# The last block of a mixture-of-experts feed-forward: its rows leave memory, and a gate matrix takes them to their tokens

## The chip, the cores and the metric

The kernel runs on one core of a Trainium2 chip. A core has a matrix engine (TensorE, PE in the profile; PEld is its loading of the stationary operand), a vector engine (VectorE, DVE), an activation engine (ScalarE, ACT), a general engine that also issues the indirect transfers (GpSimd, POOL), and a queue that issues plain transfers (SyncE, SP). Each engine works through its own list of instructions in order; between engines there are semaphores. The metric is the device time of one execution in microseconds; a time is given as the median of several executions. A profiled execution also leaves a trace, in which every instruction has its start, its length and what it waited for.

## What is computed

Two layers work on an image batch of 4 images with 384 channels and 32x32 pixels, that is 1024 tokens for each image. Layer 0 is a convolution-like attention with relative positions, followed by a small feed-forward. Layer 1 is a depthwise convolution, followed by a mixture of experts; only this end matters here:

```python
t = _to_tokens(x)                      # (4, 1024, 384)
t = t + _L1_ffn_ref(_ln_t(t), ...)
x = _from_tokens(t, x)                 # back to (4, 384, 32, 32)

def _L1_ffn_ref(x, gate_w, gate_b, w1, b1, w2, b2):      # 4 experts, top 2
    probs = softmax(x @ gate_w + gate_b)
    masked = probs with only the two largest kept, divided by (their sum + 1e-9)
    h = gelu(einsum('bsd,edh->ebsh', x, w1) + b1)        # 384 -> 1536
    y = einsum('ebsh,ehd->ebsd', h, w2) + b2             # 1536 -> 384
    return einsum('bse,ebsd->bsd', masked, y)
```

So each token's result is its own value plus gate0 times the row that its first expert made of it, plus gate1 times the row of its second expert. The kernel computes only the two chosen experts of each token.

## The kernel before, in words

Layer 0 (the first 1700 us) is left out here; the change touches nothing of it.

**Sorting tokens to experts.** For each image, `gates` and `scatter` choose two experts per token, give each pair of token and expert a slot in the expert's list in memory, and write the normalised token row there (`xs_d`). The lists are cut into blocks of 128 rows. There are 67 blocks (`ALL`), in four groups of 13, 16, 16 and 22 that follow the four images: a group starts when the image that completes its blocks has been sorted.

**Blocks.** `blocks(g, more)` runs the blocks of a group, one after the other. For each block, GpSimd gathers its 128 rows (`xg`, line 1265) and, where they change, the expert's weights (`w`, line 1284); TensorE turns the rows (`turn`, line 1278). Then come 12 steps `ff`: three products of 128x128 with the first weight (line 1316), GELU on ScalarE (line 1319), and, two steps later, one product of 128x384 with the second weight into the sum `py` (line 1294). Every float32 product is two instructions on TensorE. When the twelfth second product is done, VectorE adds the bias (`yo`, line 1297) and SyncE writes the 128 rows to `y_d` in memory (line 1299). Since the second products run two steps late, block k's `yo` is made during the second step of block k+1.

**Work beside the blocks.** After each step `blocks` calls `more(g, k)`, which issues pieces of other work. In the last group, from block 6 on (`NOT_LAST`), this is `combine(range(3))`: it works out for every token of all four images in which rows of `y_d` its two results lie (`result_rows`, which writes them as unsigned integers to `images[b]["pos"]`), and then finishes the first three images in pieces of 256 tokens, 12 in all.

**Bringing results back to tokens.** For a piece, `results` issues four gathers on GpSimd (line 1355; two for each half of 128 tokens, one per expert choice, into `rows` buffers, of which there are 16); `weigh` multiplies the first by its gate on ScalarE (line 1367) and adds gate times the second on VectorE (line 1368); `finish` turns the result by six transposes of 128x128 on TensorE (line 1344), adds it to the image on VectorE in two instructions (line 1345), and writes 256 tokens to the output (line 1346).

**The end.** `combine([B - 1])`, the fourth image, runs after all 67 blocks. Its 16 gathers are issued at once and may read any row of `y_d`, so the first of them waits until the last block's rows have been written. The image itself (`xbs[3]`) is still in on-chip memory.

**What sets the order.** The code is a trace of instructions; a planner orders each engine's list afterwards by the times of a model, free to move what is ready earlier ahead of what was written earlier. `pin` takes that freedom away: it keeps an instruction behind whatever was written just before it for the same engine. The tiles of a pool with the same tag share a fixed number of buffers (`bufs`); an instruction that needs one waits until its last reader is done. In PSUM there are two banks of tag `m`, three of `h`, two of `y` and one of `t`.

Of the kernel before, what the change touches and what calls it, by code (L numbers as in the profile page):

```python
# [53 lines left out]
MAXB = B * N // BLK  # L54
OUTSIDE = 1e6
# [749 lines left out]
def result_rows(nc, small, image, pieces):  # L805
# [18 lines left out]
    nc.vector.tensor_copy(image["pos"], row)  # L824

# [78 lines left out]
def rest_phase(tc, cst, x, ao_d, ins, xs_d, y_d, x2_d, out):  # L904
# [9 lines left out]
    with ExitStack() as es:  # L914
# [344 lines left out]
        def blocks(g, more):  # L1259
# [32 lines left out]
            def second(k, ff, hs, w, py):  # L1292
                o = WB + ff % FH * C
                nc.tensor.matmul(py, hs, w[:, o : o + C], start=(ff == 0), stop=(ff == NF - 1))  # L1294
                if ff == NF - 1:
                    yo = hid.tile([P, C], F32, tag="yo", name="yo", bufs=2)
                    nc.vector.tensor_tensor(yo, py, w[:, WB + FH * C :], ALU.add)  # L1297
                    n = (g["start"] + k) * BLK
                    nc.sync.dma_start(y_d[n : n + BLK, :], yo)
# [30 lines left out]

        def combine(bs):
# [4 lines left out]
            y_rows = y_d if end else y_d[: (groups[-1]["start"] + NOT_LAST) * BLK]  # L1336
            pieces = [p for g in groups for p in g["pieces"]]

# [9 lines left out]
            def results(b, n0):  # L1348

                zs = []  # L1350
                for j in range(2):
                    ys = [new_row() for _ in range(2)]
                    for i, y in enumerate(ys):
                        index = images[b]["pos"][:, n0 // P + j, i : i + 1]
                        nc.gpsimd.indirect_dma_start(y, None, y_rows, bass.IndirectOffsetOnAxis(ap=index, axis=0))
# [8 lines left out]
            def weigh(b, n0, zs):  # L1364
                for j, (z, y) in enumerate(zs):
                    gate = images[b]["gate"][:, n0 // P + j, :]
                    nc.scalar.activation(z, z, AF.Copy, scale=gate[:, 0:1])
                    nc.vector.scalar_tensor_tensor(z, y, gate[:, 1:2], z, ALU.mult, ALU.add)
                return [z for z, _ in zs]

            if not end:
                for b in (*bs, B - 1):
                    result_rows(nc, small, images[b], pieces)
                    yield 3.0, 0.0
            todo = [(b, n0) for b in bs for n0 in range(0, N, w)]
            ahead = {}
            for i, (b, n0) in enumerate(todo):
                for more in todo[i : i + (len(todo) if end else 2)]:
                    if more not in ahead:
                        ahead[more] = results(*more)  # L1380
                zs, xr = ahead[b, n0]
# [5 lines left out]
                finish(b, n0, xr, zs)  # L1387
# [101 lines left out]
        def more(g, k):  # L1489
# [4 lines left out]
            spend(g.get("combined", iter(())))  # L1494
            while clock[0] < clock[1] and spend(todo):
# [7 lines left out]
        for _ in groups[-1]["combined"]:  # L1503
            pass
        for _ in combine([B - 1]):
# [103 lines left out]
```

## Time and profile before

| what | value |
|---|---|
| time, three executions | 3046.1, 3054.85 and 3057.67 us; median 3054.85 |
| the profiled execution's own time | 3037.78 us |
| its span in the profile | 3036.0 us, so 1.78 us lie around it |
| busy share of the span | PE 96%, DVE 65%, ACT 45%, POOL 38% |
| one block of the last group, without other work beside it | 16.3 us (from one `yo` to the next, 2972.81 and 2989.11) |
| the second last block's `yo` starts | 2989.11 us |
| the last block's `yo` starts | 3003.56 us |
| from there to the end | 32.4 us |

The page of a profile has a table of busy times, a strip of 40 slices of the span, the chain of work that ended last, and groups of like instructions. In a group the columns are: source line, engine, operation, output and inputs with their shapes, count, total busy time and mean length in ns, idle time of the engine before it and what ended that. A query for stretches of time gives, for each stretch, its length, the busy time and count of each engine, the clock that TensorE was granted (1.00 is full speed), and the transfers.

### The profile page before, as it was taken

To read this page: it belongs to the slowest core of one execution; us is meant where nothing else is said; L and a number is where in the kernel's file an instruction comes from. 1 tells how busy PE (TensorE), PEld (TensorE's weight loads), DVE (VectorE), ACT (ScalarE), POOL (GpSimd) and SP (SyncE) were. 2 spreads that over 40 slices of the span, in tenths; PEclk is the share of its full clock that TensorE was granted. 3 is DMA by queue.
4 is the path that set the end of the run, shared out by engine and by line. 5 is a ranking of instruction groups with operands and counts; after the bars stand their busy time and mean duration, and the time that the engine had idled before them with its cause. 6 is when DMAs were issued, how large, how long until landed. Compare 5 with 4: busy or idle time off the path is not lost.

```text
span 3036.0 us, 63460 instructions
## 1 busy us (share of the span) xinstructions
PE 2914.2 (96%) x25391; PEld 2017.5 (66%) x25391; DVE 1960.5 (65%) x3577; ACT 1370.9 (45%) x2833; POOL 1156.4 (38%) x1123
## 2 busy tenths in 40 slices
PE   9998999999999999999999789999999999999996
PEld 4555777777777777777533347776577777778774
DVE  3237787778787878787578869999999740001101
ACT  1116667666666666666422232332343242233332
POOL 1115656464747373747400123252024322115412
PEclk9999999999999999999999879999999999999998
DMA  4346667667666666665500304734144056366752
GB/s 156 138 139 216 153 217 163 217 160 213 169 206 176 205 168 205 168 209 156 195 21 35 135 27 159 273 144 156 65 159 158 28 189 235 134 254 245 281 190 73
DMA packets 274568, 500.56 MB, mean 165 GB/s; under 512 B 135632, under 2 KB 204112, under 8 KB 266592
## 3 DMA queue, kind: packets, MB, share of 16 engines
q1 hardware_dynamic: 185376, 269.93, 28.8%
q0 software_dynamic: 37792, 202.68, 18.0%
q10 hardware_dynamic: 51104, 23.89, 3.9%
q8 instruction: 200, 3.28, 0.5%
q14 instruction: 96, 0.79, 0.1%
HBM read 543.58 MB, written 152.37 MB: 229 GB/s over the span
## 4 chain that ended last, share of the span: by engine, by line
PE 74%; DVE 11%; issue 8%; DMA 3%; POOL 2%; ACT 2%; SPq 0%; ACTq 0%; POOLq 0%; DVEq 0%
PE e_ps L1316 14%; PE y_ps L1294 13%; PE t_ps L408 7%; PE av_ps L221 7%; PE sc_ps L221 7%; DVE xb L1104 6%; PE tabq_ps L221 5%; PE qk_ps L174 4%; PE a_ps L418 3%; PE v_ps L185 2%; PE tv_ps L221 2%; PE tap_ps L1152 1%; DVE extra L400 1%; PE row_ps L87 1%; POOL bias L351 1%
## 5 line engine op out<-in xcount | busy, mean ns | idle before, releaser
L1316 PEld LDWEIGHTS e_ps<-xT,w 128*128 128x128 f32 x4824 | 655.1, 192 | 213.6 <-issue 11.5
L351 POOL TENSOR_TENSOR bias<-b,s 128x416 f32<-128x416 f32 (+24 forms) x656 | 659.8, 1042 | 183.3 <-DMA s<-sd 165.1
L1316 PE MATMUL e_ps<-xT,w 128*128 128x128 f32 x4824 | 669.1, 276 | 10.6 <-DVE xb L1045 4.0
L1294 PE MATMUL y_ps<-w,eh 128*128 128x384 f32 x1608 | 649.1, 489 | 5.3 <-ACT eh L1319 5.0
L1104 DVE SCALAR_TENSOR_TENSOR xb<-img,pack,xb 128x1024 f32<-128x1024 f32 (+1 forms) x539 | 634.6, 1243 | 0.0
L1319 ACT ACTIVATE eh<-e_ps,w 128x128 f32<-128x128 f32 x804 | 293.8, 367 | 706.1 <-PE e_ps L1316 694.5
L1284 POOL DMA_INDIRECT w<-in_w,row x134 | 170.5, 1273 | 720.5 <-PE y_ps L1294 273.3
L400 DVE TENSOR_REDUCE extra<-arow 128x32 f32<-128x32 f32 (+24 forms) x768 | 381.0, 554 | 8.6 <-ACT arow L389 4.9
L379 DVE CUSTOM_DVE_ANT_0 arow<-sc_ps,bias 128x1024 f32<-128x1024 f32 x256 | 312.5, 1221 | 103.6 <-issue 55.1
L389 ACT ACTIVATE arow<-arow,nm 128x1024 f32<-128x1024 f32 x256 | 302.2, 1181 | 77.9 <-DVE nm L379 68.9
L408 PEld LDWEIGHTS t_ps<-ident,arow 128*128 128x128 f32 x2048 | 220.0, 142 | 174.5 <-ACT aT L409 100.5
L409 ACT COPY aT<-t_ps 128x512 f32<-128x512 f32 x512 | 278.4, 603 | 92.6 <-PE t_ps L408 92.1
L408 PE MATMUL t_ps<-ident,arow 128*128 128x128 f32 x2048 | 281.8, 281 | 16.7 <-ACT arow L389 16.7
L1297 DVE TENSOR_TENSOR yo<-y_ps,w 128x384 f32<-128x384 f32 x67 | 37.1, 554 | 386.1 <-PE y_ps L1294 386.1
L221 PE MATMUL sc_ps<-kk,qs 48*32 48x512 f32 x4096 | 277.5, 605 | 7.3 <-DVE nm L379 6.0
L1294 PEld LDWEIGHTS y_ps<-w,eh 128*128 128x128 f32 x1608 | 247.7, 192 | 17.8 <-ACT eh L1319 7.1
L221 PEld LDWEIGHTS av_ps<-aT,vb 128*64 128x64 f32 x4096 | 222.3, 137 | 51.3 <-ACT aT L409 42.1
L316 DVE STREAM_TRANSPOSE b<-tabk_ps 128x480 f32<-128x480 f32 x256 | 218.5, 982 | 35.1 <-PE tabk_ps L221 35.0
L221 PE MATMUL av_ps<-aT,vb 128*64 128x128 f32 x4096 | 237.7, 274 | 0.0
L221 PE MATMUL tabq_ps<-tab,kq 48*128 48x480 f32 x512 | 219.5, 578 | 4.7 <-ACT st L320 2.6
L221 PE MATMUL tabk_ps<-tab,kq 48*128 48x480 f32 x512 | 222.6, 582 | 0.0
L221 PEld LDWEIGHTS tabq_ps<-tab,kq 48*128 48x128 f32 x512 | 148.6, 296 | 44.4 <-ACT aT L409 5.4
(210 smaller groups left out, 3138.1 us busy)
## 6 DMA issues: line engine op xcount, KB each, us to landing
sd<-st SPq DMA_DIRECT2D x128, 480.0 KB, 2.5
s<-sd SPq DMA_DIRECT2D x256, 240.0 KB, 4.0
xs_d<-zero SPq DMA_DIRECT2D x64, 384.0 KB, 4.4
tvw<-in_tv SPq DMA_DIRECT2D x120, 192.0 KB, 4.3
y_d<-yo SPq DMA_DIRECT2D x67, 192.0 KB, 2.1
qk_d<-qk_sb POOLq DMA_DIRECT2D x48, 256.0 KB, 2.4
qs<-qk_d SPq DMA_DIRECT2D x256, 48.0 KB, 3.0
kq<-qk_d ACTq DMA_DIRECT2D x56, 192.0 KB, 4.5
```

The costliest lines, as they stand in the source:

```text
L221: ins = nc.tensor.matmul(*args, **kw)
L316: turn = nc.vector.transpose(b2.rearrange("p e y x -> p x (e y)")[:, i + j], ps[:, j, : SPAN * IMG])
L351: nc.gpsimd.tensor_tensor(bias[:, y0:y1, :], bass.AP(b2.tensor, b2.offset + (e * IMG + y0) * IMG, [list(b2.ap[0]), [(step * IMG + 1) * IMG ...
L379: nc.vector.tensor_tensor_reduce(s["flat"], ps.rearrange("p h n -> p (h n)"), s["bias"].rearrange("p y x -> p (y x)"), -SCALE, BIG, ALU.ad ...
L389: nc.scalar.activation(s["flat"], s["flat"], AF.Exp, bias=s["nm"], scale=-1.0, accum_out=dn[:, y % YT : y % YT + 1])
L400: pin(nc.vector.tensor_reduce(ex[:, i, :], a[:, p0:p1, :].rearrange("p y x -> p x y"), AX.X, ALU.add))
L408: pin(nc.tensor.transpose(pt[:, j, :], s["flat"][:, k0 : k0 + P], ident))
L409: pin(nc.scalar.copy(aT[:, 4 * g : 4 * g + 4, s["y"] % YB, :], pt))
L1104: ins_ = nc.vector.scalar_tensor_tensor(acc[:, k, y0:y1], img[:, k, dy + y0 : dy + y1, dx : dx + IMG], w7[:, k, dy, dx : dx + 1], acc[:, k ...
L1294: nc.tensor.matmul(py, hs, w[:, o : o + C], start=(ff == 0), stop=(ff == NF - 1))
L1316: nc.tensor.matmul(ph, w[:, o : o + P], xT[k][:, c, :], start=(c == 0), stop=(c == KC - 1))
L1319: nc.scalar.activation(hs, ph, AF.Gelu, bias=w[:, o : o + 1])
```

## The change

The rows of the last block (block 66, rows from `LAST` = 8448 on) are no longer written to `y_d`. They stay on chip as `yo`, and reach their tokens of the fourth image through a matrix product.

- `choose` builds the matrix `picked` (128 block rows by 1024 tokens). For each 128 tokens, VectorE compares the two row numbers of each token, less `LAST`, with 0 to 127 and multiplies by the gate (two instructions of 128x128), adds the two (one more), TensorE turns the result (one transpose), and ScalarE copies it from PSUM into the part of `img` that the convolution no longer needs. It is advanced by one step for each of the 12 pieces of the first three images.
- `kept` holds the fourth image's gates, with zero where the row lies in the last block.
- The 16 gathers of the fourth image read `y_d[:LAST]` with a check on the bound (an index beyond it moves nothing). They are issued when the second last block has handed out its `yo`, that is, during the second step of the last block, no longer after the last block.
- `weigh` of the fourth image uses `kept`, and both its instructions are pinned.
- `close` takes the place of `finish` for the fourth image: three products of `yo` (128x128) with 256 columns of `picked`, then six products of the weighed rows with the identity that add to the same three banks (of tags `m`, `h` and `y`), three additions of 128x256 on VectorE, and the write.

```diff
+LAST = (ALL - 1) * BLK
@@ result_rows
     nc.vector.tensor_copy(image["pos"], row)
+    return row
@@ blocks, second
                     nc.vector.tensor_tensor(yo, py, w[:, WB + FH * C :], ALU.add)
                     n = (g["start"] + k) * BLK
-                    nc.sync.dma_start(y_d[n : n + BLK, :], yo)
+                    g["result"] = k, yo
+                    if n < LAST:
+                        nc.sync.dma_start(y_d[n : n + BLK, :], yo)
@@ new
+        kept = small.tile([P, nj, 2], F32, tag="e_kept", name="e_kept", bufs=1)
+        picked = img.rearrange("p k y x -> p (k y x)")[:, :N]
+        def choose(row):
+            gate = images[B - 1]["gate"]
+            rel = small.tile([P, nj, 2], F32, tag="e_rel", name="e_rel", bufs=1)
+            nc.vector.tensor_scalar_add(rel, row, -float(LAST))
+            nc.vector.tensor_scalar(kept, rel, 0.0, None, ALU.is_lt)
+            nc.vector.tensor_tensor(kept, kept, gate, ALU.mult)
+            line = small.tile([P, P], F32, tag="e_line", name="e_line", bufs=1)
+            for n0 in range(0, P, MAXB):
+                nc.vector.tensor_scalar_add(line[:, n0 : n0 + MAXB], pc["blocks"], float(n0))
+            yield
+            last = None
+            for j in range(nj + 1):
+                if last is not None:
+                    ps = ps_m.tile([P, P], F32, tag="m", name="pick_ps")
+                    nc.tensor.transpose(ps, last, ident)
+                    nc.scalar.copy(picked[:, (j - 1) * P : j * P], ps)
+                if j < nj:
+                    hits = [small.tile([P, P], F32, tag=f"e_hit{i}", name="e_hit") for i in range(2)]
+                    for i, hit in enumerate(hits):
+                        nc.vector.tensor_scalar(
+                            hit, line, rel[:, j, i : i + 1], gate[:, j, i : i + 1], ALU.is_equal, ALU.mult
+                        )
+                    last, other = hits
+                    nc.vector.tensor_tensor(last, last, other, ALU.add)
+                yield
@@ combine
-            y_rows = y_d if end else y_d[: (groups[-1]["start"] + NOT_LAST) * BLK]
+            y_rows = y_d[:LAST] if end else y_d[: (groups[-1]["start"] + NOT_LAST) * BLK]
+            def close(b, n0, xr, zs):
+                yo = groups[-1]["result"][1]
+                sums = []
+                for c, (pool, tag) in enumerate(((ps_m, "m"), (ps_h, "h"), (ps_y, "y"))):
+                    ps = pool.tile([P, TOK], F32, tag=tag, name="out_ps", **({"bufs": 2} if tag == "y" else {}))
+                    nc.tensor.matmul(
+                        ps[:, :w], yo[:, c * P : (c + 1) * P], picked[:, n0 : n0 + w], start=True, stop=False
+                    )
+                    sums.append(ps)
+                for j in range(2):
+                    for c, ps in enumerate(sums):
+                        nc.tensor.matmul(
+                            ps[:, j * P : (j + 1) * P], zs[j][:, c * P : (c + 1) * P], ident,
+                            start=False, stop=(j == 1),
+                        )
+                for c, ps in enumerate(sums):
+                    nc.vector.tensor_tensor(xr[:, c, :], xr[:, c, :], ps[:, :w], ALU.add)
+                nc.sync.dma_start(out[b, :, n0 : n0 + w].rearrange("(k p) n -> p k n", p=P), xr)
@@ combine, results
-                        nc.gpsimd.indirect_dma_start(y, None, y_rows, bass.IndirectOffsetOnAxis(ap=index, axis=0))
+                        bound = {"bounds_check": LAST - 1, "oob_is_err": False} if end else {}
+                        nc.gpsimd.indirect_dma_start(
+                            y, None, y_rows, bass.IndirectOffsetOnAxis(ap=index, axis=0), **bound
+                        )
@@ combine, weigh
-                    nc.scalar.activation(z, z, AF.Copy, scale=gate[:, 0:1])
-                    nc.vector.scalar_tensor_tensor(z, y, gate[:, 1:2], z, ALU.mult, ALU.add)
-                    gate = images[b]["gate"][:, n0 // P + j, :]
+                    gate = (kept if end else images[b]["gate"])[:, n0 // P + j, :]
+                    keep = pin if end else lambda ins_: ins_
+                    keep(nc.scalar.activation(z, z, AF.Copy, scale=gate[:, 0:1]))
+                    keep(nc.vector.scalar_tensor_tensor(z, y, gate[:, 1:2], z, ALU.mult, ALU.add))
@@ combine, the loop over pieces
+                chooser = choose(row)
...
+                if end and not i:
+                    yield 0.0, 0.0
+                elif not end:
+                    next(chooser, None)
...
-                finish(b, n0, xr, zs)
+                (close if end else finish)(b, n0, xr, zs)
@@ more
+            if g is groups[-1] and g.get("result", (0,))[0] == g["nb"] - 2 and "tail" not in g:
+                for _ in g["combined"]:
+                    pass
+                g["tail"] = combine([B - 1])
+                next(g["tail"])
@@ after the groups
-        for _ in groups[-1]["combined"]:
-            pass
-        for _ in combine([B - 1]):
+        for _ in groups[-1]["tail"]:
             pass
```

More of the change, by code (lines that the diff above doesn't have):

```diff
@@ L1372, in combine @@
                 for b in (*bs, B - 1):
-                    result_rows(nc, small, images[b], pieces)
+                    row = result_rows(nc, small, images[b], pieces)
                     yield 3.0, 0.0
+                chooser = choose(row)
             todo = [(b, n0) for b in bs for n0 in range(0, N, w)]
```

## The prediction

> **What bounds the kernel now.** I read the page's strip first, then the chain of work that ended last over the final 50 us, then the busy times by stretch, then the groups of the stage in which the new preparation lies. The strip says that TensorE is nearly always busy, so the end of the kernel is the place to look for time in which it is not:
>
> ```profile
> PE   9998999999999999999999789999999999999996
> PEclk9999999999999999999999879999999999999998
> ```
>
> ```profile
> 3001.58 1.96 PE y_ps L1294 x6
> 3003.53 0.02 issue
> 3003.56 0.57 DVE yo L1297
> 3004.14 1.85 DMA y_d<-yo
> ...
> 3006.06 0.71 issue
> 3006.77 0.97 POOL rows L1355
> 3007.74 0.30 issue
> 3008.05 0.97 POOL rows L1355
> ...
> 3026.27 3.29 DMA rows<-y_d,pos
> ...
> 3029.66 0.63 DVE rows L1368
> 3030.28 0.04 issue
> 3030.33 0.92 PE out_ps L1344 x3
> 3031.27 0.69 DVE xb L1345
> ```
>
> This is the chain. Until 3003.5 it is TensorE. Then it is one line: yo is added, its write lands, and GpSimd issues 16 gathers, one every 0.97 + 0.30 us; the last starts to land at 3026.27, and after it come one VectorE, one TensorE and one more VectorE step and the write, to 3036.0. What is done to the gathered rows (lines 1367, 1368, 1344) hides between the gathers, but for the last piece.
>
> ```profile
> 2986.00:3003.00 17.00, 17.00 (x102) 13.16 (x101) 0.56 (x1) 4.89 (x13) 0.00 (x0) 1.00 0.04 13
> 3003.00:3011.00 8.00, 0.52 (x2) 0.00 (x0) 0.56 (x1) 0.61 (x1) 3.31 (x4) 0.84 0.26 77
> 3011.00:3019.00 8.00, 2.23 (x8) 1.28 (x8) 2.93 (x6) 1.84 (x3) 6.17 (x7) 0.50 0.57 156
> 3019.00:3027.00 8.00, 3.42 (x12) 1.89 (x11) 2.59 (x5) 1.84 (x3) 6.17 (x7) 0.50 0.82 241
> ```
>
> Busy times by stretch (columns PE, PEld, DVE, ACT, POOL, clock, DMA share, GB/s): during the last block, 2986 to 3003, GpSimd does nothing and the DMA engines are 4% busy. Afterwards GpSimd is the full engine, and TensorE's clock falls to 0.50.
>
> **What it removes: 14.45 us.** The gathers now need the yo of the second last block, not of the last. The chain before shows 3006.77 - 3003.56 = 3.21 us from the start of yo to the first gather; the second last yo starts at 2989.11, so the first gather starts at 2992.3, and all 16 move forward by 3003.56 - 2989.11 = 14.45 us. Is the queue free? GpSimd's last other instruction is a weight gather at 2974.14 (1.00 us); the `rows` buffers were read last by the third image's transposes (they end by 2906.3); the row numbers are done by 2524 (line 824). SyncE has only the write of that yo to issue. Nothing waits behind the gathers on GpSimd, since block 66's rows and weights are asked for during block 65. The dropped write of the last yo (1.85 us) is part of the 14.45 and isn't counted again. No more can be won: from 3003.56 on, the last block's own result has its products, additions and write ahead of it.
>
> **What it adds to the gathers: +0.85 us.** They get a bound check. The nearest rows are the block gather `xg`, the same 128x384 rows with a check (median 1012 ns), and the gathers without (956 ns): 0.056 us for each of 15 intervals. Bounds: 0, as the intervals are no longer for xg's issue gap of 0.30; and 15 x 0.15 = 2.3 us, if they run like the slowest quarter (1.16 and 1.33 occur). I take the xg row, the nearest.
>
> **What it adds beside the blocks: +1.1 us.** The groups of 2735 to 2910, where it is written (the row numbers, written there too, were moved up to 2490 to 2524, so the gate matrix may move up as well; TensorE is as full from there on):
>
> ```profile
> L1316 PE MATMUL e_ps<-xT,w 128*128 128x128 f32 x720 | 97.3, 275 | 2.0 <-ACT xT L1279 1.7
> L1344 PE MATMUL out_ps<-ident,rows 128*128 128x128 f32 x72 | 10.4, 274 | 1.9 <-DVE rows L1368 1.9
> L1345 DVE TENSOR_TENSOR xr<-xr,out_ps 128x256 f32<-128x256 f32 x12 | 5.0, 415 | 0.0
> ```
>
> TensorE is the bound there, so the 8 new transposes lie on the path: 10.4/72 = 0.144 us each, 1.1 us; bounds 0 (TensorE has gaps, about 4 us between 2815 and 2915, into which they could fall) and 8 x 0.274 = 2.2 us, none overlapped. VectorE's part, 24 instructions of 128x128 at some 0.285 us (its 128x128 rows: 283 to 286 ns) = 6.9 us and a handful of small ones, is free: VectorE is busy 2.7 to 4.5 us in each 20 us there. So are the 8 copies on ScalarE, at 0.37 us each (its 128x128 GELU row, 367 ns): it is idle two thirds of the time, and second products run two steps behind. If that cover failed, each would hold TensorE by up to 0.37, 3.0 us in all. SP gets nothing here, GpSimd neither.
>
> **After the last block: +0.7 us.** For each piece, TensorE now has three products of 128x256 in two instructions each and six of 128x128 in two each, where it had six transposes. Before the end, the chain gives 0.67 us for six instructions of 128 columns (0.111 each) and 0.65 for two of 384 (0.324 each), so 256 cost about 0.217: 3 x 2 x 0.217 + 6 x 2 x 0.111 = 2.6 us a piece at full clock, 5.3 at half. The pins chain VectorE's list: the second piece's `weigh` stands behind the first piece's additions. A piece thus takes, from yo on, two weighings (2 x 0.62), three products of the second half (0.67), and the rest of three additions (3 x 0.415 less what overlaps, about 0.85), near 3.0 to 3.5 us. The gathers deliver a piece every 4 x 1.32 = 5.3 us. Now in shifted times (1.1 later): yo is ready at 3005.2; piece 0 is done by 3008.7, piece 1 by 3012.2; piece 2's last gather lands around 3011.5, so it is done by 3015.5; piece 3's last gather starts at 2993.4 + 15 x 1.32 = 3013.2 and lands at 3016.6. The gathers still set the end, narrowly. After the last landing there follow a weighing, three products in six instructions (0.67 at full clock, 1.33 at half) where three transposes took 0.92, and three additions of 0.415 of which the last two or three are exposed, where 0.69 and 0.33 were. That is -0.25 to +0.41 for the first, 0 to +0.4 for the second; I take +0.2. If the clock falls on the way, a piece takes 1.3 us longer (0.66 in each half's products); from piece 2 on this would hold the last piece by about 1.0, and I take half, +0.5. Bounds: -0.2, and +7 if all four pieces run at half clock from the start: 4 x 5.3 = 21.2 us of TensorE from 3005.2 is 3026.4, against 3019.5 if the gathers pace it.
>
> The clock is what I can't read off. Before, it is 0.84 in the first 8 us after the blocks and 0.50 from then on, with TensorE 28 to 43% busy. In the change TensorE is about 70% busy in that stretch and starts out at 1.00, so the first two pieces should run at full clock. The Trainium skill, in "TensorE: Matmul & The Clock Gate", Part 1, says that the clock halves after an idle window of about 3.4 us and comes back after a busy one; in Part 4, that transposes don't count as busy for it. The trace's 0.50 under transposes agrees with both. By that rule the new identity products, which are no transposes, would hold the clock up, and the +0.5 would be 0; its warning against idle gaps over 3 us would bite between pieces 2 and 3 alone.
>
> **Sum.** -14.45 + 0.85 + 1.1 + 0.7 = -11.8 us. The profiled execution takes 3037.78 us (its span of 3036.0 and 1.78 around it), so it becomes 3026.0. That execution lies 17.07 us under the median of the three runs, 3054.85, though the end of the kernel is the same program; I carry the difference over: 3043.0 us.
>
> **Rivals.**
>
> 1. *TensorE, at half clock, paces the end* (21.2 us from yo, as above), or the 8 transposes are moved by the planner to the end, where each with its copy would cost up to a microsecond. For: 0.50 throughout the end before. Against: it starts at full clock. The gain shrinks to about 5 us: 3050.
>
> 2. *Slower: the gate matrix stalls the blocks.* TensorE takes its list in order. If the planner puts a transpose right behind its three VectorE instructions, and these stand in VectorE's list behind a weighing (line 1368) that waits for a gather, TensorE stands still until the gather lands. The gathers land in 4.3 us at the median and 10.8 at worst, so one stall could cost 6.5 us, and eight of them 52. Against: the transposes of `finish` hang on the same gathers, and they cost TensorE 1.9 us in all, in two waits, the longest 1.3; each gate transpose is written one piece, some ten steps, after its VectorE part, and if the planner moves it up before 2735 there is no gather to wait for. It eats the gain at 11.8/8 = 1.5 us a stall. At 3.5 us a stall, 28 us, the kernel takes 3071; the point for slower by over 0.5% is 3.4.
>
> 3. *The gathers don't run beside the block*, because something else holds them: a `rows` buffer, or a wait that the planner adds. Then only the write of the last yo is saved, about 2.6 us from yo's end to the first gather, against +2 added: 3054. Against: the list of holders above, all done by 2992.
>
> 4. *The planner's order changes as a whole.* The new chain alters what it thinks urgent, and other stalls come or go in 1300 us of mixed work. TensorE idles some 4% of the span. Either sign; about 20 us: 3035 or 3075.
>
> **How the numbers follow.** No difference under 0.5%, 15.3 us, can be told well from none here: the three runs alone spread over 11.6 us, so a median moves by some 5 us. Forecast 0.70; rival 1 0.10; rival 2 0.07; rival 3 0.03; rival 4 0.10, in which 0.06 go faster. The forecast's true gain lies between 9 and 14 us, 3.5 us from that bound at its centre, and with the scatter I give it 0.45 of reading beyond. Faster: 0.70 x 0.45 + 0.06 = 0.38. Slower: 0.07 + 0.03 = 0.10 (rival 2 nearly always past its point, most of rival 4's other side). The rest, 0.52, is within. The forecast's own range is 3034 to 3051. For 8 in 10 the range must take in rivals 1 and 3 on the upper side with their scatter and the scatter of a lucky low: 3031 to 3060.
>
> **What the profile after would show.** Right: in the stretch of the last block GpSimd is busy from about 3 us after the second last yo (some 8 gathers before the last yo); gathers of 1.01 us; no wait for a write of `y_d` after the last block; 19 to 20 us from the last yo to the end, not 32.4. Rival 1: full use of TensorE at 0.50 after the last block, with gathers long landed. Rival 2: TensorE waits on the gate matrix's VectorE line before 2910. Rival 3: the first gather after the last yo. Rival 4: the last yo itself comes more than 4 us away from 3003.6. The prediction falls if the blocks lose more than the 2.2 us of the new transposes, or if the first gather of the last image doesn't start by about 2995.

## The result: no measurable change, and the profile after

The changed kernel takes 3055.98 us (median of 22 executions, 3047.58 to 3066.36), the kernel before 3053.75 on the same chip (22 executions, 3046.1 to 3062.84): a ratio of 1.0004, 95% interval 0.9995 to 1.0013. The time lies in the predicted range of 3031 to 3060 and on the side that got the largest chance, but above the forecast's own 3034 to 3051: the gain of 11.8 us behind the number didn't come. The profiled execution of the changed kernel took 3053.67 us, with a span of 3051.9.

Differences in us below are of medians, unless a ratio is given. First the page's strip after, which answers the one shown of before: TensorE is busy for eight tenths of the last slice in place of six, at nine tenths of the clock in place of eight. The end is fuller, and no shorter.

```profile
PE   9998999999999999999899789999999999999998
PEclk9998999999999999999999879999999999999999
```

The busy times by stretch around the last block (columns: stretch, length, PE, PEld, DVE, ACT, POOL, granted clock, DMA share, GB/s). The last two `yo` start at 3011.80 and 3031.08.

```profile
2995.00:3012.00 17.00, 17.00 (x105) 13.34 (x104) 0.75 (x2) 5.18 (x14) 1.00 (x1) 1.00 0.04 13
3012.00:3020.00 8.00, 8.00 (x51) 6.40 (x51) 0.36 (x1) 2.21 (x6) 3.69 (x4) 1.00 0.31 85
3020.00:3028.00 8.00, 6.27 (x33) 4.18 (x32) 0.00 (x0) 2.23 (x6) 6.17 (x7) 1.00 0.53 148
3028.00:3036.00 8.00, 4.51 (x15) 3.77 (x15) 1.61 (x3) 2.99 (x6) 6.17 (x7) 0.64 0.53 148
3036.00:3044.00 8.00, 7.28 (x43) 6.17 (x43) 4.28 (x10) 0.61 (x1) 0.20 (x1) 0.93 0.35 117
```

The change does what it says: GpSimd's 16 gathers run beside the last block, from 3015.40, 3.60 us after the second last `yo`, and they cost 1014 ns each by their group, the check included. But TensorE, full until 3020, isn't full after that: the last block has not ended when the gathers are half through. The chain of the end shows it:

```profile
3023.60 0.67 PE e_ps L1320 x6
3024.27 2.52 PE y_ps L1296 x4
3026.87 0.38 ACT eh L1323
3027.29 0.91 PE y_ps L1296 x2
3028.21 3.48 issue
3031.69 2.92 PE out_ps L1380 x6
3034.62 3.64 PE out_ps L1386 x12
```

The 3.48 us stand between the last product with a weight, done at 3028.21, and the first with `picked`, which needs the last `yo`. VectorE makes that `yo` late (in brackets its idle time before, and what ended it; "remote" is a releaser that the profile can't tell):

```profile
3031.08 0.56 DVE L1299 TENSOR_TENSOR yo<-y_ps,w 128x384 f32<-128x384 f32 x1 [18.72 <-remote]
```

It comes 19.27 us after the `yo` before it; in the kernel before, it came 14.45 us after.

The rest of the loss lies more than a thousand microseconds earlier. The first `yo` of all starts at 1842.0, against 1834.2 before. The lists of VectorE and of GpSimd at the start of the second half of the kernel, from the output projection of layer 0 on (start, busy time, engine, line, operation, shapes, count; like instructions in a row stand in one line) show where:

```profile
1497.87 9.15 DVE L1348 TENSOR_SCALAR e_line<-pack 128x32 f32<-128x32 f32 x4
1506.93 0.16 DVE L98 RECIPROCAL s_rstd<-s_rstd 128x4 f32<-128x4 f32 x1
1507.13 0.69 DVE L116 TENSOR_TENSOR s_dg<-ident,s_rstd 128x512 f32<-128x512 f32 x1
```

```profile
1495.96 10.85 POOL L1136 TENSOR_TENSOR w<-half,pack 128x3136 f32<-128x3136 f32 x2
```

The four additions that make `e_line`, part of `choose`, need only constants. The planner moved them up a thousand microseconds, into the first 1700 us, which the part on the kernel before says the change doesn't touch: to the place where VectorE normalizes the first image behind the projection. GpSimd makes two long products there. Two of the four additions took 0.17 us; the other two took 3.58 and 5.48, and they end at 1501.44 and 1506.84, where GpSimd's products end (1501.40 and 1506.81). The normalization, on which TensorE waits, stands behind them, and the chain of work that ended last runs through them:

```profile
1497.95 9.06 DVE e_line L1348 x4
```

Two theories from here. **A**: the `e_line` additions hold VectorE at 1498, and without them the sum of the prediction comes true. **C**: gathers beside the block disturb the block by as much as they save. **B**, for what neither explains: this one execution was slow.

### The profile page after: what moved, and what is told of

Same layout as the page of the kernel before. It is cut to its first block, busy times and chain, and to the rows that moved or that the text cites. A ratio compares the mean times of both kernels' runs of the same rounds, so it can differ in the third digit from the quotient of the medians.

```text
span 3051.9 us, 63617 instructions
## 1 busy us (share of the span) xinstructions
PE 2928.4 (96%) x25447; PEld 2027.3 (66%) x25447; DVE 1975.4 (65%) x3612; ACT 1372.6 (45%) x2841; POOL 1157.9 (38%) x1123
## 4 chain that ended last, share of the span: by engine, by line
PE 72%; DVE 14%; issue 6%; DMA 3%; POOL 2%; ACT 2%; SPq 0%; ACTq 0%; another core or an unknown queue 0%; DVEq 0%; POOLq 0%
PE e_ps L1320 12%; PE y_ps L1296 12%; DVE xb L1106 8%; PE t_ps L409 7%; PE av_ps L222 7%; PE sc_ps L222 7%; PE tabq_ps L222 6%; PE qk_ps L175 4%; PE a_ps L419 3%; PE v_ps L186 2%; PE tv_ps L222 2%; DMA s<-sd 2%; PE tap_ps L1154 1%; PE f_ps L1029 1%; PE o_ps L1033 1%
```

## Experiments

Of each profile I use four lengths: from the first projection of the second half (line 992 or 994) to the first `yo`; from the 36th `yo` to the 61st (blocks beside the scatter and the combination of earlier images); from the second last `yo` to the last; from the second last `yo` to the end, which takes in the one before. What they leave out differs less: 1482.6 to 1490.0 us up to the first projection, 656.5 to 658.9 from the first `yo` to the 36th, 84.7 in every profile from the 61st to the second last. All profiles of the study, by the starts of those instructions; "chip" gives before's median on the chip of that run:

| profile | chip | to the first `yo` | 36th to 61st | last two `yo` | second last to the end | span |
|---|---|---|---|---|---|---|
| before | - | 351.5 | 412.9 | 14.45 | 46.90 | 3036.0 |
| before_again | 3040.65 | 352.8 | 413.2 | 14.45 | 47.25 | 3040.6 |
| before_third | 3041.09 | 351.2 | 413.1 | 14.45 | 46.43 | 3035.8 |
| before_fourth | 3040.57 | 351.8 | 413.0 | 14.44 | 46.76 | 3036.7 |
| before_fifth | 3062.36 | 347.6 | 432.4 | 14.45 | 46.87 | 3052.8 |
| the change | 3053.75 | 358.9 | 428.2 | 19.27 | 40.07 | 3051.9 |
| after_again | 3059.83 | 355.1 | 431.8 | 22.99 | 42.45 | 3055.7 |
| e1_line_later | 3040.65 | 351.3 | 414.3 | 14.45 | 34.11 | 3024.4 |
| e1_again | 3059.83 | 351.4 | 429.9 | 25.15 | 44.06 | 3050.9 |
| e2_line_alone | 3040.65 | 363.7 | 413.2 | 14.45 | 46.75 | 3050.7 |
| e3_gathers_late | 3040.65 | 351.4 | 414.7 | 14.45 | 48.64 | 3042.8 |
| e3_again | 3041.09 | 354.0 | 414.5 | 14.45 | 47.54 | 3046.4 |
| e4_product_in_pieces | 3059.83 | 364.7 | 431.0 | 25.52 | 44.14 | 3066.3 |
| e5_later_and_pieces | 3059.83 | 363.4 | 433.9 | 26.25 | 46.19 | 3076.4 |

(before's own first profile has no such median beside it; 3062.36 and 3040.57 are single executions.)

**1. The additions later.** The four additions are bound to an instruction of the last image's scores, a thousand microseconds later, where they are first of use.

```diff
-        def choose(row):
+        def choose(row, behind):
...
-            for n0 in range(0, P, MAXB):
-                nc.vector.tensor_scalar_add(line[:, n0 : n0 + MAXB], pc["blocks"], float(n0))
+            with tc.issue_after(behind):
+                for n0 in range(0, P, MAXB):
+                    nc.vector.tensor_scalar_add(line[:, n0 : n0 + MAXB], pc["blocks"], float(n0))
...
+                    behind = latest(mybir.EngineType.DVE)
...
-                chooser = choose(row)
+                chooser = choose(row, behind)
```

> The changed kernel, with the four additions that fill e_line queued on VectorE behind the row numbers of the last image, so that they can no longer be moved up into the start of the second half of the kernel, where they run beside a long product on GpSimd. Theory A (they hold VectorE there until GpSimd's product ends, 7.4 us of the path): 7 to 8 us faster than the changed kernel, so about 3048.5, 0.998 of the kernel before; the first yo starts at about 1834, not 1842. Rival B (the 7.8 us are scatter between executions; the profiled execution of the kernel before was 16 us under its median): no change against the changed kernel, 1.000 of before.

Measured: 3029.29 us against 3040.65, a ratio of 0.9966 (0.9954 to 0.9979), so 11.4 us less. The first `yo` stands at 1834.1, and the tail is the predicted one. Its chain from the second last `yo`:

```profile
2990.31 0.57 DVE yo L1299
2990.89 1.85 DMA y_d<-yo
...
3011.18 1.01 POOL rows L1412
3012.19 0.30 issue
3012.50 4.77 DMA rows<-y_d,pos
3017.29 0.62 ACT rows L1427
3017.94 0.63 DVE rows L1428
3018.57 0.04 issue
3018.61 0.74 PE out_ps L1387 x2
3019.38 0.42 DVE xb L1392
```

Gathers end to end set the end, as the prediction had it; the last block, whose `yo` is at 3004.75, isn't on this chain at all. Its clock by stretch, 2987 to 3020:

```profile
2987.00:3004.00 17.00, 17.00 (x103) 13.26 (x102) 0.56 (x1) 5.65 (x15) 7.96 (x8) 1.00 0.31 88
3004.00:3012.00 8.00, 7.35 (x45) 6.30 (x44) 4.83 (x12) 2.60 (x5) 6.17 (x7) 1.00 0.60 176
3012.00:3020.00 8.00, 5.16 (x31) 4.33 (x30) 4.03 (x10) 1.23 (x2) 2.21 (x3) 0.92 0.65 197
```

From the second last `yo` to the end it is 34.11 us, where the four undisturbed profiles of before have 46.43 to 47.25.

**2. The additions alone.** The kernel before, with only the four additions, at the top of `combine`; nothing reads their result.

```diff
+        line = small.tile([P, P], F32, tag="e_line", name="e_line", bufs=1)
+        for n0 in range(0, P, MAXB):
+            nc.vector.tensor_scalar_add(line[:, n0 : n0 + MAXB], pc["blocks"], float(n0))
```

> The kernel before, with only the four additions that fill e_line, which nothing reads; nothing else of the change. Theory A: 7 to 8 us slower than before (1.0024), with two e_line additions of some 3.6 and 5.5 us that end with GpSimd's two products. Rival B: within 1 us of before.

Measured: 3048.33 us, a ratio of 1.0021 (1.0006 to 1.0036, that is 1.8 to 10.9 us), 7.7 us more, of the expected size. But the profile doesn't show what was expected. The additions were short this time. They and other early instructions changed places with each other, and it was two others that stood:

```profile
1497.50 0.49 DVE L1333 TENSOR_SCALAR e_line<-pack 128x32 f32<-128x32 f32 x4
...
1500.40 3.31 DVE L844 SCALAR_TENSOR_TENSOR b_slot<-done,pack 128x4 f32<-128x4 f32 x1
...
1503.86 5.79 DVE L115 TENSOR_TENSOR s_dg<-ident,s_rstd 128x512 f32<-128x512 f32 x1
```

```profile
1498.25 10.85 POOL L1134 TENSOR_TENSOR w<-half,pack 128x3136 f32<-128x3136 f32 x2 [0.30 <-POOL pack L749]
```

`b_slot` has 4 elements per partition and takes 0.17 us elsewhere; here it takes 3.31 and ends at 1503.71, where the first product ends (1498.25 + 10.85/2 = 1503.68). So it isn't `e_line` as such. Whichever of these VectorE instructions is due while a product runs stands until that product ends; one more or less ahead decides which one meets it, and how often. Before has one such stall too: its `s_dg` takes 1.99 us at 1499.38, in place of 0.69, and ends 0.55 us behind GpSimd's first product; the second product then takes 5.90 us in place of 5.44.

**3. The gathers late.** The first experiment, but the last block's rows are written, and the gathers wait for them; the product with the gate matrix stays, and is now superfluous work.

```diff
-                    if n < LAST:
-                        nc.sync.dma_start(y_d[n : n + BLK, :], yo)
+                    nc.sync.dma_start(y_d[n : n + BLK, :], yo)
...
-            y_rows = y_d[:LAST] if end else y_d[: (groups[-1]["start"] + NOT_LAST) * BLK]
+            y_rows = y_d if end else y_d[: (groups[-1]["start"] + NOT_LAST) * BLK]
...
-                next(g["tail"])
```

> The first kernel of this batch (e_line later), but the last block's rows are written to memory as before and the 16 gathers wait for that write; the product with the gate matrix stays. Theory A (the gathers beside the last block save what the prediction says): 13 to 15 us slower than the first of this batch, about 3062, 1.0027 of before. Rival C (the gathers beside the block disturb the block by as much as they save: in the changed kernel's profile the last block's end is 7 us late): only 5 to 8 us slower than the first of this batch.

Measured: 3044.83 us, a ratio of 1.0015 (1.0005 to 1.0026) to before, and 15.5 us over the first experiment. On this chip gathering beside the block is worth what it was predicted to be worth, and C falls, here. Of the last image's gate product only its cost is left in this kernel: 4.2 us over before (1.5 to 7.9).

**4. Before once more**, to see whether its profile is always as smooth.

> The kernel before once more, for a second profile of it. If the stalls of 1 to 4 us that the changed kernel shows between 2490 and 2910 (a product that waits for a GELU, which waits for TensorE) are scatter, this profile has such stalls too, some 10 to 15 us in all, at a span of about 3050. If they come from the change, it has none, and its last yo starts within 2 us of 3003.6 plus what lies before 1834.

Measured: 3042.34 us, and in the table the lengths of the first profile within 1.3 us, with no late stalls. By its expectation they would then belong to the change; but the first experiment, which has all of the change but the place of four additions, shows none either, which spoke for B.

That would have closed the case as A and B. The second set took it apart.

**5. The change and the first experiment again, on one chip.**

> The change as it is, for a second profile of it and beside the others on one chip. Theory A (VectorE's e_line adds are held by GpSimd's long products at the start of the second half, 7.4 us of the path) and theory B (what the first profile of the change showed between 2490 and 2910 us and in the last block was that one execution, not the change): the first yo is again 6 to 9 us later than before's 1834, e_line again takes about 9 us in all, and after it the distances between the yo are before's within 1 us per image; the time is 10 to 15 us above e1's. If the late stalls belong to the change (rival to B), they come again at the same products and the last yo is once more over 20 us later than before's.

> The e_line adds behind the block of the last image's scores, once more, on the same chip as the change itself, so that the two can be set against each other. Theory A: 10 to 15 us under the change, 10 to 13 us under before. Rival (the earlier chip favoured it): less than 5 us under before.

Measured, on a chip where before takes 3059.83 us: 3059.45 us for the change (ratio 1.0001, 0.9990 to 1.0012) and 3055.60 for the version with late additions (0.9991, 0.9982 to 1.0001). The difference of the two means is 4.6 us, with an interval of 3.0 to either side, not 10 to 15, and against before it is the rival's outcome, less than 5 us. The four additions of the change take 8.8 us again, as expected, but its first `yo` is 4.9 us later than 1834.1, not 6 to 9. The late stalls of the first profile are back, in every kernel that was profiled on this chip: B falls. ScalarE's list in the last block of e1_again, then three lines of TensorE and VectorE:

```profile
3014.16 0.37 ACT L1323 ACTIVATE eh<-e_ps,w 128x128 f32<-128x128 f32 x1 [0.96 <-PE e_ps L1320]
3015.47 0.37 ACT L1323 ACTIVATE eh<-e_ps,w 128x128 f32<-128x128 f32 x1 [0.95 <-PE e_ps L1320]
3017.76 0.37 ACT L1323 ACTIVATE eh<-e_ps,w 128x128 f32<-128x128 f32 x1 [1.92 <-PE e_ps L1320]
3020.63 0.37 ACT L1323 ACTIVATE eh<-e_ps,w 128x128 f32<-128x128 f32 x1 [2.50 <-PE y_ps L1296]
3025.60 0.37 ACT L1323 ACTIVATE eh<-e_ps,w 128x128 f32<-128x128 f32 x1 [4.61 <-remote]
```

```profile
3018.49 0.83 PE L1320 MATMUL e_ps<-xT,w 128*128 128x128 f32 x6
...
3026.02 1.65 PE L1296 MATMUL y_ps<-w,eh 128*128 128x384 f32 x2 [4.06 <-ACT eh L1323]
...
3032.01 0.56 DVE L1299 TENSOR_TENSOR yo<-y_ps,w 128x384 f32<-128x384 f32 x1 [24.60 <-remote]
```

TensorE's products for these five start every 1.31 us, the last at 3018.49, and take 0.83 us each; a GELU follows its product's start by 0.92. Here the last three follow by 1.9, 3.5 and 7.1. VectorE has the same: the last `yo` starts at 3032.01, though the product that it adds began at 3026.02 and took 1.65. What is late is the word from TensorE that a product is done: the semaphore on which these GELUs wait rises at 3017.68, 3020.55 and 3025.52 in the trace, 1 to 6 us behind the products. What holds it up the profile doesn't say; nor does it show whether the products themselves end late, since their ends are modelled. It begins 7 us after the first gather at 3010.45. Here the last two `yo` are 25.15 us apart, and the tail gains 46.87 - 44.06 = 2.8 us in place of 12.7. The measured gain is 4.2 by the medians, 2.8 by the ratio.

**6. GpSimd's products in pieces.** If an addition stands until *the* product that it met ends, short products should cost less. The order of all other instructions is unchanged.

```diff
-                nc.gpsimd.tensor_tensor(
-                    diag[k], bcast(half.unsqueeze(1), 1, 49),
-                    bcast(w7[:, k].rearrange("p y x -> p (y x)").unsqueeze(2), 2, 64), ALU.mult,
-                )
+                taps = w7[:, k].rearrange("p y x -> p (y x)").unsqueeze(2)
+                for t in (slice(t0, t0 + 7) for t0 in range(0, 49, 7)):
+                    by = bcast(taps[:, t], 2, 64)
+                    nc.gpsimd.tensor_tensor(diag[k][:, t], bcast(half.unsqueeze(1), 1, 7), by, ALU.mult)
```

In the change itself, and in the first experiment's version:

> The change, with each of GpSimd's two products of 128x3136 made in seven pieces of 128x448; the order of every engine's other instructions is the same, e_line stands where the change has it. Theory A (an e_line add that meets a running product is held until that product ends): a piece takes 5.44/7 = 0.78 us, so e_line is held at most 0.78 us at a time, four times: at most 3.6 us in all in place of 9.15, the first yo comes 5 to 8 us earlier than in the change's profile, and the time is 5 to 9 us under the change's. Rival D (e_line is late for another reason: its place in VectorE's order, or its operands): e_line takes 9 us as before, the time is the change's within 1.5 us. A cost of the pieces themselves (12 more GpSimd instructions) would show in the taps' products, which read them: an end of the last piece more than 1.5 us later than 1506.8.

> The e_line adds behind the last image's scores, and the products in seven pieces each. Theory A: what is left of the hold in e1 is s_dg's 2.13 us in place of 0.69; it falls to at most 1.5, the rest stays: the time is e1's to 1.3 us less, too little to tell apart. Rival D: e1's time. If the pieces cost anything by themselves, it is longer than e1's by that.

Measured: 3065.45 us, 6.0 over the change (means: 4.8, with 3.7 to either side), and 3063.56 us, 8.0 over the first experiment's version (8.7, with 4.2). Both expectations are missed, D's too. The sign that was named for a cost of the pieces themselves did come: the last piece ends at 1508.7, 1.9 us behind 1506.8. Lists of the change in pieces, GpSimd and VectorE:

```profile
1496.13 12.56 POOL L1139 TENSOR_TENSOR w<-half,pack 128x448 f32<-128x448 f32 x14
```

```profile
1498.47 10.51 DVE L1348 TENSOR_SCALAR e_line<-pack 128x32 f32<-128x32 f32 x4
```

One addition took 10.26 us and ended with the *fourteenth* piece. In the other kernel it is `s_dg`, which in the first experiment took 2.13:

```profile
1507.17 9.07 DVE L116 TENSOR_TENSOR s_dg<-ident,s_rstd 128x512 f32<-128x512 f32 x1
```

It ends at 1516.2, GpSimd's last piece at 1515.7. So it is shown that the VectorE instruction stands because of GpSimd's products, since only these were altered and the stall grew with them; and A was wrong in one point: the end of a product isn't enough to let VectorE in. Between the two products of 5.44 us it got in, between pieces of 0.90 us it didn't. What makes the difference is open: the trace shows no gap in either stream, each product or piece starting some 0.03 us before the one ahead of it ends. How much of the 4.8 us is the longer stall (10.51 us for the four additions, in place of 9.15 and 8.8) and how much the later end of the pieces isn't told apart either.

**7. Does before have the late hand-overs too?** Three more profiles of before, and the third experiment again, on whatever chip came.

> The kernel before, for one more profile. On the last chip the version with the late e_line adds gained only 2.8 us (11.4 on the chip before it), and its trace showed what the change's first trace showed: GELUs that start 1.5 to 4.6 us after their product is done, between 2496 and 2910 us and in the last block, each time while GpSimd's scatters or gathers of rows are on their way. Theory C, mended (on a chip that does this, rows moved by GpSimd make the hand-over from TensorE to ScalarE late, whoever issues them): if this chip does it, before shows the late GELUs between 2496 and 2910 too, the yo there are 12 to 20 us later than in before's first profile, and its last block, beside which it gathers nothing, is undisturbed: 14.4 us between the last two yo. Rival E (only the change's kernels suffer, because of their own instructions): before shows none. On a chip that doesn't do it, neither shows and nothing is told apart.

> The late e_line adds, with the last image's gathers after the last block once more (its rows are written and gathered, the product with the gate matrix stays). Theory C, mended: the last block is undisturbed on any chip (14.4 us between the last two yo), and the time stands to before as on the first of these chips, 0 to 7 us above it; with e1 at 2.8 us under before on the disturbed chip, the gathers beside the block are worth 3 to 10 us there in place of 15.5. Rival E (the lost 8.6 us of e1 lie elsewhere, in its picks or its product): on a disturbed chip e3 is 12 us or more above before.

> The kernel before, once more, since the chip of the last call showed no late GELUs. Theory C, mended: on a chip that shows them, they come in before too between 2496 and 2910 us (the yo there 12 to 20 us later than in before's first profile), and not in its last block, 14.4 us between the last two yo. Rival E: before shows none on any chip, and its longer time on such a chip comes from elsewhere.

> The kernel before, a last time, for the same question: where late GELUs are to be had, theory C, mended, expects them in before between 2496 and 2910 us, the yo there 12 to 20 us later than in before's first profile, with an undisturbed last block (14.4 us between the last two yo); rival E expects none in before on any chip.

The first two of these chips were undisturbed and told nothing on that; e3_again took 3043.96 us on one, a ratio of 1.0009 (0.9997 to 1.0021), as in the third experiment. The last was a disturbed one: before at 3062.36 and 3054.60 us. ScalarE's list of before_fifth, beside the first gathers of `combine`, from 2737.64 on:

```profile
2742.11 0.37 ACT L1319 ACTIVATE eh<-e_ps,w 128x128 f32<-128x128 f32 x1 [0.25 <-ACT xT L1279]
2744.13 0.37 ACT L1319 ACTIVATE eh<-e_ps,w 128x128 f32<-128x128 f32 x1 [1.66 <-PE e_ps L1316]
2747.68 0.37 ACT L1319 ACTIVATE eh<-e_ps,w 128x128 f32<-128x128 f32 x1 [3.18 <-PE e_ps L1316]
2751.94 0.63 ACT L1319 ACTIVATE eh<-e_ps,w 128x128 f32<-128x128 f32 x2 [3.90 <-remote]
```

From the 36th to the 61st `yo` it takes 432.4 us, 19.5 more than the 412.9 of the first profile, and its last two `yo` are 14.45 apart: its last block has no gathers beside it. Behind the 36th `yo`, 15 of its GELUs start more than 1.9 us after the start of their product; in the other four profiles of before none does. E falls, and C, mended, holds: on some chips a block beside which GpSimd moves rows is held up, in both kernels, and the change puts the last block among them. That the changed kernel's last block would be undisturbed on such a chip without the gathers wasn't seen, since the third experiment met none; before_fifth shows it for before.

What stays open is what makes it late. Not each burst of GpSimd's transfers does: the scatter from 1981 to 2011 in before_fifth is beside blocks whose times are those of the other chips. Its 16 transfers come one each 2.0 us, the disturbing ones one each 1.3; whether that is the reason wasn't tried. And the weight gathers alone, 2525 to 2735, don't make it late either.

## Why the prediction was right and where it was wrong

**-14.45 us, the gathers earlier: right in mechanism, and in size on an undisturbed chip.** The first gather starts 3.30 to 3.60 us after the second last `yo` (predicted 3.21), in every profile that has it early. In e1_line_later the way from there to the end is 34.11 against 46.84 (mean of before's five): -12.7 us, where the three terms that belong there, -14.45 + 0.85 + 0.7, give -12.9. The step that fails is the one that holds the last block's own length fixed while the gathers run beside it ("Now in shifted times (1.1 later): yo is ready at 3005.2", and from that "The gathers still set the end"). On disturbed chips this block takes 19.3, 23.0 and 25.2 us in the change and e1_again, its `yo` comes late and sets the end, and the same sum is then worth 6.8, 4.4 and 2.8 us.

**+0.85 for the bound check:** 1.01 to 1.02 us each as predicted, 19.9 us from the first gather to the last in e1_line_later against 18.9 to 19.5 of before, so +0.4 to +1.0.

**+1.1 for eight transposes:** 414.3 to 414.7 in the three profiles of changed kernels on undisturbed chips, against 412.9 to 413.2, so +1.1 to +1.8. Right, with no stall behind a weighing: rival 2 didn't come. The groups of the change between 2735 and 2925 (line, engine, operation, tiles, count, busy us and mean ns, idle us before and what ended it):

```profile
L1399 PE MATMUL out_ps<-ident,rows 128*128 128x128 f32 x66 | 9.3, 273 | 1.3 <-DVE rows L1427 1.3
...
L1354 PE MATMUL pick_ps<-ident,e_hit 128*128 128x128 f32 x8 | 2.6, 321 | 0.7 <-DVE xr L1400 0.7
```

The eight new transposes (`pick_ps`) waited 0.7 us in all, and not for their own matrix.

**VectorE's part "is free": wrong**, and the term that spoils the sum on both kinds of chip. Not the 24 instructions of 128x128, but the "handful of small ones": four additions of 128x32, which nobody was waiting for. The way to the first `yo` is 358.9 and 355.1 us in the two profiles of the change. Without them at that place, and with GpSimd's products whole, nine profiles have 347.6 to 354.0, in the mean 351.4: so some 3.6 to 7.4 us more, with a scatter of 3 to either side. By the time it is 4.6 us (1.6 to 7.6) between the change and the first experiment on one chip, and 7.7 for the additions alone on another. The prediction asked whether the planner would move the gate matrix up, and looked only at how full the engines are there; it didn't ask what an instruction with no inputs but constants does at the earliest place it can go. It is rival 4 in small: four early instructions and not the whole order. The sign of rival 4, a last `yo` more than 4 us away from 3003.6, came (3031.08), by this and by the late blocks.

**The end, +0.7:** right as a sum where the last block is undisturbed: from the start of the last gather to the end e1_line_later has 10.61 us, before's five profiles 9.73 to 10.30 (3026.27 in the prediction's chain is the start of that gather; it landed 3.29 us later). Not all of its parts are: from the last weighing on VectorE to the end it is 6.48 against 6.35 to 6.37, and the rest lies ahead of that weighing. From the last block's `yo` to the end it is 19.67, and 20.80 in the change, where 19 to 20 were predicted. Rival 1, half clock throughout, didn't come: in e1_line_later the clock is 1.00 until 3018.7 and 0.50 from there, which is what the 0.92 of the last stretch is made of. Two like groups of products, one ahead of that point and one across it:

```profile
3015.85 0.94 PE L1387 MATMUL out_ps<-ident,rows 128*128 128x128 f32 x6 [1.01 <-DVE rows L1428]
...
3018.61 1.58 PE L1387 MATMUL out_ps<-ident,rows 128*128 128x128 f32 x6 [1.83 <-DVE rows L1428]
```

So the 0.64 us for the slower products of one half did come. The rule of the Trainium skill that was weighed against the trace ("TensorE: Matmul & The Clock Gate", Parts 1 and 4) had the larger part right, since products with the identity ran at full clock through three pieces. But the prediction read it to mean that the clock would hold but for idle gaps over 3 us, and here it fell behind waits of 1.01 and 1.83 us with 0.94 us of work between them.

**Carrying the 17.07 us over** as scatter was the second wrong step. It was taken to fall on the kernel alike, before and after. But executions of one kernel on one chip spread over 16 to 18 us, and the chips differ by as much: before_fifth's extra 19.5 us lie in nine of the 25 blocks from the 36th `yo` to the 61st. The prediction was made from a profile without them, for a chip that by its times has them: before's median there is 3053.75, and the change's profile has 428.2 us in these blocks. The prediction was to fall if the blocks lost more than 2.2 us, or if the first gather didn't start by about 2995; by that profile the blocks lost 15, though not to the transposes it had in mind, and the first gather started at 3015.40.

So on the chip of the result, as far as the profile goes and with before's lengths taken from other chips, since it wasn't profiled there: -6.8 in the tail, +7.4 before the first `yo`, +1.3 for the transposes, which is about 2 and near what was measured (+2.2 by the medians, -1.5 to +4.0 by the ratio). On the chip of after_again the same account gives -4.4 + 3.6 + 1.3 = +0.5, with -0.4 measured. Two errors, one of 4 to 7 us and one of 6 to 10 on disturbed chips, used up the gain. That "same" got the largest chance is owed to the scatter, which was to hide a gain of 9 to 14 us in 0.55 of the cases; that it came out with no gain at all is luck, and not the forecast's reason.

The Trainium skill, "SBUF — State Buffer", section "Who interferes with whom", says that a VectorE instruction with two SBUF inputs, or a `tensor_scalar` in a 2-port mode, contends with GpSimd, and that whoever issues first holds the shared pair "for the whole instruction" while the other fully blocks. The trace agrees with the kind: `e_line`, `b_slot` and `s_dg` stood, and statistics read from PSUM and fills beside them didn't. It differs in how long: with pieces of 0.90 us the wait was 10.26 us, to the end of the last piece and not of one.

## What to carry to other kernels

An instruction that is ready early isn't free because its engine has idle time: a planner puts it as early as it can, and there it may meet another engine. Tie it to the place where it is needed; here that is worth some 4 to 8 us, and the version with these additions tied is faster than before on an undisturbed chip (0.9966, 0.9954 to 0.9979) and equal to it or a little faster on a disturbed one (0.9991, 0.9982 to 1.0001). The change itself was never measured on an undisturbed chip.

Work moved beside a block is paid for only if the block's own length stays: take that length from the trace, on more than one chip, and see from a profile with and one without whether it does.

## What the runs showed of the hardware

- A VectorE instruction of two inputs, or an addition of a constant, that met GpSimd's elementwise products stood: 3.58 and 5.48 us with two products of 5.44, each time until one of them ended; 10.26 us with fourteen of 0.90, until the last of them ended. Cutting the GpSimd work into pieces made it worse.
- Chips differ not only by a percentage over the whole kernel. On some, the hand-over from TensorE to ScalarE and VectorE came 1 to 6 us late while GpSimd's gathers or scatters were under way (7.1 us in place of 0.92 at worst, from a product's start to its GELU), with the granted clock still at 1.00 (2738 to 2752 in before_fifth); on others the same program showed none. It makes 19.5 us in nine of 25 blocks of the kernel before. The cause is open.
